# An fp32 attention block: the last product of each four-group stream moved one half block, and the last additions issued singly

## The chip, the cores and the metric

The kernel runs on one core of a Trainium2 chip. The metric is the device time of one execution in microseconds (us); before the change it is 3124.0 us, the median of three runs between 3122.99 and 3124.39.

## The reference, cut to what matters

The input is 16 images of 512 channels by 1024 positions, fp32. Each is normalised in 8 groups of channels, goes through one projection to q, k and v, attention with 4 heads of 128 channels, an output projection and the residual.

```python
xn  = groupnorm(x, 8) * gamma + beta              # x: (16, 512, 32, 32)
q, k, v = split(einsum('oc,bchw->bohw', qkv_w, xn) + qkv_b, 3)
attn = softmax(einsum('bhnd,bhmd->bhnm', q, k) * dh ** -0.5)
out  = einsum('bhnm,bhmd->bhnd', attn, v)          # 4 heads of dh = 128
return x + einsum('oc,bchw->bohw', proj_w, out) + proj_b
```

## The kernel before, in words

**Blocks and half blocks.** The spine of the program is a loop over 16 images x 4 heads x 8 key blocks. Each key block is done in two halves of 512 queries, called half blocks here. A half block issues one product of scores (tile `s`, line 1674, in `score`), its exponential on ScalarE (tile `p`, line 1680), and the weighted sum of the previous block (tile `po`, line 1771). VectorE adds up the exponentials once per block (tile `tot`, line 1695). A head has 16 half blocks, numbered 0 to 15.

**What runs between them.** All other products are put into these half blocks as units: one entry of the list `halfway` is run behind the `po` product of each half block. They are the q/k products of the next images, the v products, and the output projection of the image before (head 1, tiles `pp`). They use Strassen's scheme on two levels. Seven outer products are made in four groups (`OUTER = ((1, 5), (2, 6), (7, 4), (3,))`), and each group is a Strassen scheme of seven inner units in the order p1, p2, p6, p5, p7, p4, p3. From image 4 on, q, k and v come from another scheme instead (`thirds`, 16 groups, tiles `t_x`, `t_y`, `t_z`, line 1241), so four-group streams remain for the projection of every image but the last (15 of them), for v of images 1 to 3 (head 3 of the image before), and for the q/k products of images 1 to 3: the first pair in head 2 of the image before (stride 4), the second pair in head 0 (stride 3).

**The y bank.** Inside a group, p5 makes the bank y and p7 the bank x; VectorE adds both into the group's result (`out_`, line 817, here the first reading addition). Only then may p3 add its product onto y; VectorE reads y again behind it (the second reading addition, line 817). p3 of the last group is one instruction, `pp_y<-o` in the projection, 128 x 256.

**The order around the change.** `paced` puts the seven units of group g at the half blocks `stride * g + (0, 1, 1, 2, 2, 3, stride)`. With stride 3 and four groups the last entry is 12, and it holds both p4 and p3 of the last group:

```python
for k, i in enumerate((0, 1, 1, 2, 2, 3, stride)):
    at = halves_[stride * g + i]
    at.insert(1 if k == 0 and len(at) > 1 else len(at), us[k])
if stride == 4:
    carry.append(halves_.pop())
```

**Additions of whole blocks.** When a group is complete, `combine` queues additions of its results in the list `pending`. Each unit gives out one of them; in the last group of everything but v it gives out two; `end` gives out the rest. In the projection an output block (c11, c22, c21, c12) is finished by `finish`: the residual tile `y_c` plus one result (line 1648), plus the other (line 1649), then a DMA to the output on POOL's queue (line 1650). In v, `finish` is a VectorE scalar operation (line 1039), then `turn_v`: a transpose on VectorE (line 1046), a DMA to a scratch row, and four DMAs back. The tiles for these come from a pool of two.

**The next stream.** Head 2, behind the projection, starts `thirds` of the next image (from image 4 on). Its first group needs sums that VectorE makes in `home_A` (line 1159), its p3 is `t_y<-x`, and the second group's p2 is `t_z<-f`. ScalarE copies `t_x` into `t_z` (line 659) ahead of that p2. In the same stretch ScalarE issues the DMA of the softmax denominators (`row<-r`, line 1743), which waits for VectorE's reciprocal (line 1723).

Of the kernel before, what the change touches and what calls it, by code (L numbers as in the profile page):

```python
# [181 lines left out]
OUTER = ((1, 5), (2, 6), (7, 4), (3,))  # L182
# [49 lines left out]
def fast_path(ctx, tc, x, sources, out, consts, flag, dims):  # L232
# [6 lines left out]
    nc = tc.nc  # L239
# [150 lines left out]
    def own_t4(name="ot4"):  # L390
        t = tpool.tile([P, KC, HALF], F32, tag="ot4", name=name)
        return t
# [224 lines left out]
    ahead, inner_kept, late = {}, {}, {}  # L617

    def run(units):
        for u in units:  # L620
            u()
# [75 lines left out]
    def two_levels(name, site, b, blocks, finish, sums="make", homes="BBBB", prepare=None):  # L697
# [9 lines left out]
        opening = b == 0 and site == 0  # L707

        def placed():
            return tc.high_priority(URGENT) if opening else nullcontext()  # L710

        def part(g, i, row=None):
            t = R[g][:, i]
            return t if row is None else t[:, row, :]
# [42 lines left out]
        def group_units(g):  # L757
            group = OUTER[g]
            n = len(group)
# [82 lines left out]
            def unit(*steps):  # L842
                def one():
                    for f in steps:
                        f()
                    with placed():
                        for _ in range(min(len(pending), 2 if g == len(OUTER) - 1 and site != "v" else 1)):
                            pending.pop(0)()
                return one

            def end():
                combine(g)
                if g == len(OUTER) - 1:
                    with placed():
                        run(pending)
                    pending.clear()


# [9 lines left out]
                    first_keys if opening and g == len(OUTER) - 1 else lambda: None,  # L868
                ),
                unit(lambda: load("t3"), p4), unit(lambda: load("t4"), p3, end),  # L870
            ]

# [14 lines left out]
        pending = []  # L887
# [8 lines left out]

        def done(which, i, j):
            if prepare:
                pending.append(lambda: finish(which, part(*i), part(*j)))
                return  # L900
            pending.extend(
                lambda r=r: finish(which, r, part(*i, r), part(*j, r)) for r in range(2)
            )

        def combine(g):

            if g == 1 and opening:
                pending.append(lambda: result("c11", 0))
                add((1, 1), (0, 0), (1, 1), 0)
                add((1, 0), (1, 1), (0, 1), 0)  # L910


                def lower():
                    with tc.issue_after(latest["outer"].ins):
                        result("c11", 1)
                        nc.vector.tensor_add(part(1, 1, 1), part(0, 0, 1), part(1, 1, 1))

                pending.extend((lambda: None, lower))
            elif g == 1:
                done("c11", (0, 0), (1, 0))  # L920
                add((1, 1), (0, 0), (1, 1))
                add((1, 0), (1, 1), (0, 1))
            elif g == 2 and opening:
                add((2, 0), (1, 1), (2, 0), 0)
            elif g == 2:
                add((2, 0), (1, 1), (2, 0))
                done("c22", (2, 0), (0, 1))
                done("c21", (2, 0), (2, 1))
            elif g == 3 and opening:

                def rest():
                    result("c12", 0)
                    beside["scores"] = latest["result"]
                    with tc.issue_after(latest["result"].ins):
                        for o, i, j in (((1, 0), (1, 1), (0, 1)), ((2, 0), (1, 1), (2, 0))):
                            nc.vector.tensor_add(part(*o, 1), part(*i, 1), part(*j, 1))
                        for r in (1, 0):
                            result("c22", r)

                pending.append(rest)  # L940

                def second_head():
                    with tc.issue_after(latest["sum"].ins):
                        result("c21", 1)
                        result("c12", 1)

                beside["second head"] = second_head
            elif g == 3:
                done("c12", (1, 0), (3, 0))
# [28 lines left out]
    def qk_groups(b, pair):  # L978

        def finish(which, r, a, c):  # L980
            of, half = int(which[1]) - 1, int(which[2]) - 1
            st, h = (qs, ks)[of], 2 * pair + r
            head_tiles(b, pair)
            i = of * HEADS + h
            return nc.vector.scalar_tensor_tensor(
                st[b, h][:, ts(half, HALF)], a, qkb_sb[:, i : i + 1], c, ALU.add, ALU.add
            )

        return two_levels(
            f"qk_{b}_{pair}", pair, b, lambda: xb[b], finish,  # L990
            "make" if pair or b == 0 else "keep",
            "ABBB" if pair else "ABAB" if b > 0 else "BCBC",
        )
# [83 lines left out]
    def thirds(b):  # L1077
# [268 lines left out]
        def combine(G):  # L1346
# [88 lines left out]
            elif g == 7:  # L1435
                final(0, 0, True, 14, 13, (14, 13))
                op(True, 12, 12, 11, (11,))
                final(2, 1, False, 12, 9, (12, 9))

        return paced([group_units(G) for G in range(2 * count)], 3)  # L1440

    store3, builder = {}, {}
# [177 lines left out]
    def proj_groups(b):  # L1620

        ys = {}

        def place(which):
            row, half = int(which[1]) - 1, int(which[2]) - 1
            return lambda t: t[b, ts(row, KC * P), ts(half, HALF)].rearrange(
                "(r p) n -> p r n", p=P
            )

        def prepare(which):  # L1630
            own = which == "c12"
            t = ys[which] = own_t4(f"y_{b}_{which}") if own else ypool.tile(
                [P, KC, HALF], F32, tag="y", name=f"y_{b}_{which}"
            )
            eng = nc.sync if own else nc.gpsimd
            dma = eng.dma_start(t, place(which)(x))

            tc.add_manual_dep(
                dma.ins, last_eviction[b].ins.name,
                mybir.DependencyInfo(  # L1640
                    mybir.DependencyClass.Sync, mybir.DependencyReason.DATA
                ),
                reason="residual",
            )

        def finish(which, a, c):
            t = ys.pop(which)
            nc.vector.tensor_add(t, a, t)  # L1648
            nc.vector.tensor_add(t, t, c)  # L1649
            latest["sent"] = nc.gpsimd.dma_start(place(which)(out), t)  # L1650

        return two_levels(f"pp_{b}", "proj", b, lambda: ob[b], finish, prepare=prepare)


# [4 lines left out]
    def where(s):  # L1659
        bh, j = divmod(s, NB)  # L1660
        return (*divmod(bh, HEADS), j)
# [155 lines left out]
    def paced(groups, stride):  # L1817

        halves_ = [[] for _ in range(stride * len(groups) + 1)]
        for g, us in enumerate(groups):  # L1820
            for k, i in enumerate((0, 1, 1, 2, 2, 3, stride)):
                at = halves_[stride * g + i]
                at.insert(1 if k == 0 and len(at) > 1 else len(at), us[k])
        if stride == 4:
            carry.append(halves_.pop())
        return halves_

    def last_loads(what):
# [162 lines left out]
    def plan_head(b, h):  # L1991
# [9 lines left out]
        if h == 0:  # L2001
            if b > 0:
                if b < old:
                    spread(plan, [None] * 28, 0, NB)
                    halfway.extend(paced(next_qk.pop(), 3))
                plan[6].append(lambda: o_blocks(b - 1))
                plan[6].append(lambda: sums_of_b(ob[b - 1]))
                if old <= b < B - 1:
                    plan[5].append(lambda: load_x(b + 1, range(NCC)))
            else:  # L2010
                products(plan, staggered(next_qk.pop(), (0, 4, 8, 12)), 0)
                plan[1].append(beside["second head"])
                plan[3].append(lambda: load_x(1, range(KC)))
                for c in range(KC):
                    for half, step in enumerate(stats_steps(1, c)):
                        plan[4 + 2 * c].append(lambda step=step: behind_exp(step))
        elif h == 1:
            if b > 0:
                spread(plan, [None] * 28, 0, NB)
                halfway.extend(paced(proj_groups(b - 1), 3))  # L2020
                if flow:
                    halfway[0] = flow.pop() + halfway[0]
# [292 lines left out]
    with tc.issue_after(opened.ins):  # L2315
        run(units[3:-1])
        stage_sums(0)
        groups = [iter(units[-1:])] + [iter(us) for us in qk_groups(0, 0)]
# [13 lines left out]
    for s in range(steps + 1):  # L2332
        units = []
        if s < steps:
            b, h, j = where(s)
# [12 lines left out]
        for half in range(NH2):  # L2348
# [21 lines left out]
            n = (len(units) + 1) // 2  # L2370
# [158 lines left out]
```

## Time and profile before

| what | value |
|---|---|
| time, median of 3 runs | 3124.0 us |
| profiled execution, its own time | 3122.96 us |
| its span in the trace | 3121.4 us |
| TensorE (PE) matmul busy | 3106.9 us, 100% |
| PE weight loads busy | 2263.2 us, 73% |
| VectorE (DVE) busy | 2698.9 us, 86% |
| ScalarE (ACT) busy | 1722.7 us, 55% |
| GpSimd (POOL) busy | 469.7 us, 15% |
| one image from image 5 on | 192.75 us (the same row comes again at 1104.79 and 1297.54 us) |

The trace gives the start of each instruction, how long it was busy, and, in brackets, how long its engine had been idle before it and what ended that. One fp32 product shows as two matmul rows, so "x2" in a row of the timeline is one product. "PEld" is PE's weight load, "ACTq" ScalarE's queue, where it issues DMAs. 1.6 us of the execution lie around the span.

### The profile page before, as it was taken

What the parts mean: (1) busy time and instruction counts of PE and PEld (TensorE: products, weight loads), DVE (VectorE), ACT (ScalarE), POOL (GpSimd) and SP (SyncE); (2) the same over time, 40 slices, a digit from 0 to 9 for tenths busy, and PEclk for the clock granted to TensorE, in tenths of its full rate; (3) what the DMA queues carried; (4) which work ended last, traced back from release to release, by engine and by line L of the source; (5) the groups of instructions that cost most, each with busy time, mean ns of one, the idle gap of its engine ahead of it and who ended that gap; (6) DMA issues with size and microseconds to landing.
All of it is one profiled execution on the core that took longest, in us unless ns stands there. A gap on an engine that the chain in (4) does not pass through costs nothing.

```text
span 3121.4 us, 38228 instructions
## 1 busy us (share of the span) xinstructions
PE 3106.9 (100%) x11934; PEld 2263.2 (73%) x11934; DVE 2698.9 (86%) x4604; ACT 1722.7 (55%) x3744; POOL 469.7 (15%) x792
## 2 busy tenths in 40 slices
PE   9999999999999999999999999999999999999999
PEld 8567676677777777777777777777777777777775
DVE  9988988789898897988979889798898988989787
ACT  3545546455465655656556565565655656555543
POOL 0121121111111111211111111111111111111010
PEclk9999999999999999999999999999999999999999
DMA  5566765666767666666676666766667576675651
GB/s 177 174 227 194 249 206 192 210 196 213 235 212 221 193 209 222 205 212 198 202 221 209 212 202 204 224 202 211 200 202 230 196 219 200 210 223 191 222 194 42
DMA packets 244064, 636.80 MB, mean 204 GB/s; under 512 B 32656, under 2 KB 77840, under 8 KB 243856
## 3 DMA queue, kind: packets, MB, share of 16 engines
q1 hardware_dynamic: 164912, 363.58, 36.9%
q0 software_dynamic: 66272, 236.38, 22.3%
q10 hardware_dynamic: 12672, 34.35, 3.8%
q8 instruction: 96, 1.57, 0.2%
q14 instruction: 112, 0.92, 0.1%
HBM read 462.49 MB, written 171.69 MB: 203 GB/s over the span
## 4 chain that ended last, share of the span: by engine, by line
PE 67%; DVE 4%; issue 1%; ACT 0%; POOL 0%; ACTq 0%; DVEq 0%; POOLq 0%
PE po L1771 20%; PE s L1674 19%; PE t_x L1241 12%; PE t_y L1241 6%; PE pp_x L784 3%; PE t_z L1241 3%; PE pp_y L784 2%; PE pp_z L784 1%; DVE pp_r L817 1%; DVE pp_r L891 1%; DVE tot L1695 1%; DVE home_B L749 0%; DVE y_c L1649 0%; DVE y_c L1648 0%; DVE o L1784 0%
## 5 line engine op out<-in xcount | busy, mean ns | idle before, releaser
L1771 PE MATMUL po<-p,v 128*128 128x512 f32 x2048 | 1045.4, 592 | 0.0
L1674 PE MATMUL s<-qk,qk 128*128 128x512 f32 x2048 | 1045.2, 592 | 0.0
L1680 ACT ACTIVATE p<-s 128x512 f32<-128x512 f32 x1024 | 611.7, 597 | 509.2 <-PE s L1674 499.2
L1771 PEld LDWEIGHTS po<-p,v 128*128 128x128 f32 x2048 | 615.9, 301 | 374.9 <-issue 258.3
L1695 DVE TENSOR_TENSOR tot<-tot,p 128x1024 f32<-128x1024 f32 (+1 forms) x408 | 471.3, 1156 | 163.4 <-ACT p L1680 161.6
L1674 PEld LDWEIGHTS s<-qk,qk 128*128 128x128 f32 x2048 | 362.0, 189 | 58.9 <-issue 29.2
L1265 DVE TENSOR_TENSOR r<-t_y,t_u 128x342 f32<-128x342 f32 (+1 forms) x384 | 185.3, 482 | 138.7 <-PE t_y L1241 111.6
L1356 DVE TENSOR_TENSOR r<-r,r 128x684 f32<-128x684 f32 x264 | 225.8, 863 | 1.7
L1241 PE MATMUL t_x<-home_B,w 128*128 128x171 f32 x1008 | 187.7, 308 | 0.0
L1241 PE MATMUL t_x<-home_A,w 128*128 128x171 f32 x1008 | 187.6, 308 | 0.0
L1241 PEld LDWEIGHTS t_x<-home_B,w 128*128 128x128 f32 x1008 | 161.7, 189 | 30.2 <-issue 20.1
L1241 PEld LDWEIGHTS t_x<-home_A,w 128*128 128x128 f32 x1008 | 161.6, 189 | 30.2 <-issue 20.1
L784 PE MATMUL pp_x<-home_B,w_proj 128*128 128x256 f32 x630 | 166.0, 380 | 0.0
L1065 POOL DMA_DIRECT2D v<-vd x240 | 139.7, 589 | 148.8 <-DMA vd<-vu 55.7
L784 PEld LDWEIGHTS pp_x<-home_B,w_proj 128*128 128x128 f32 x630 | 119.2, 190 | 36.2 <-issue 12.6
L1128 DVE TENSOR_TENSOR f<-x 128x684 f32<-128x684 f32 x168 | 144.1, 858 | 0.8
L1201 ACT COPY t_u<-t_x 128x342 f32<-128x342 f32 x192 | 78.7, 410 | 119.0 <-PE t_x L1241 112.0
L293 POOL DMA_DIRECT2D x<-in_x x60 | 32.7, 548 | 640.2 <-PE t_x L1241 409.0
L1241 PEld LDWEIGHTS t_z<-f,w 128*128 128x128 f32 x528 | 89.5, 190 | 51.9 <-issue 34.3
L1326 DVE STREAM_TRANSPOSE vu<-vt 128x256 f32<-128x256 f32 x192 | 104.3, 643 | 0.0
L1207 ACT ACTIVATE t_u<-t_x,bias 128x171 f32<-128x171 f32 x192 | 72.2, 403 | 56.9 <-PE t_x L1241 56.9
L1166 POOL DMA_DIRECT2D kept_t<-home_A x96 | 52.4, 546 | 321.5 <-DVE home_A L1159 312.1
(383 smaller groups left out, 5153.7 us busy)
## 6 DMA issues: line engine op xcount, KB each, us to landing
w<-kept SPq DMA_DIRECT2D x182, 512.0 KB, 3.9
w<-kept SPq DMA_DIRECT2D x182, 384.0 KB, 4.1
kept_t<-home_A POOLq DMA_DIRECT2D x96, 342.0 KB, 3.8
home_B<-kept_t SPq DMA_DIRECT2D x96, 342.0 KB, 3.0
rinv<-row ACTq DMA_DIRECT2D x63, 512.0 KB, 4.8
x<-in_x POOLq DMA_DIRECT2D x60, 512.0 KB, 6.0
v<-vd POOLq DMA_DIRECT2D x240, 128.0 KB, 5.2
out_y<-y_c POOLq DMA_DIRECT2D x60, 512.0 KB, 3.9
```

Of the source, the lines that this page charges most:

```text
L784: latest["product"] = nc.tensor.matmul(acc[:, ts(i, Q)], have["w"][t][:, i, slot, :], inner(i, bn), start=(first and i == 0), stop=True, s ...
L1065: nc.gpsimd.dma_start(vs[b, pair][ts(q, BLK), half].rearrange("m h (k i) j -> m (h k) (i j)", k=n), rows.rearrange("(k m) (q e) -> q m k e ...
L1128: (eng.tensor_add if op == "+" else eng.tensor_sub)(made[f], of(a), of(c))
L1201: nc.scalar.copy(dst, src)
L1241: latest["product"] = nc.tensor.matmul(acc[:, ts(i, H3)], wts[G, t][:, i, slot, :], moving, start=(start and i == 0), stop=True, skip_grou ...
L1265: nc.vector.tensor_add(dst, view(a), view(c))
L1326: nc.vector.transpose(u[:, h].rearrange("p (q i j) -> p j q i", q=n, i=BLK)[:, ds(2 * q, 2)], made["vt"][:, h, ts(part, Q)].rearrange("p ( ...
L1356: (nc.vector.tensor_add if add else nc.vector.tensor_sub)(at(o), a, c)
L1674: latest["score"] = nc.tensor.matmul(sc, ks[b, h][:, ts(j, P)], qs[b, h][:, ts(half, HALF)], start=True, stop=True)
L1680: exps[s] = nc.scalar.activation(ps[s][:, ts(half, HALF)], sc, AF.Exp, scale=SCALE)
L1695: added[b, h, j] = nc.vector.tensor_add(tot[b, h][:, i], tot[b, h][:, i], ps[s][:, i])
L1771: summed = nc.tensor.matmul(po[half], v_block(b, h, j), ps[s][:, i], start=(j == 0), stop=(j == NB - 1),)
```

## The change

Four edits go together:

1. `paced`: for four groups with stride 3, p3 of the last group goes into an entry of its own, so that it runs in half block 13 instead of 12. This holds for the 15 projections, v of images 1 to 3 and the second q/k pair of images 1 to 3.
2. `done` and `finish`: in the projection the two additions of an output block are two entries of `pending` instead of one.
3. `unit`: in the last group one entry is given out per unit instead of two (the opening image keeps two).
4. `end`: what v still has pending at its end is appended to `late["tail"]`, which the main loop empties at the end of the half block, two entries each time.

```diff
-                        for _ in range(min(len(pending), 2 if g == len(OUTER) - 1 and site != "v" else 1)):
+                        n = 2 if opening and g == len(OUTER) - 1 else 1
+                        for _ in range(min(len(pending), n)):
                             pending.pop(0)()
...
                 if g == len(OUTER) - 1:
-                    with placed():
-                        run(pending)
+                    if site == "v":
+                        late["tail"] = late.get("tail", []) + pending
+                    else:
+                        with placed():
+                            run(pending)
                     pending.clear()
...
             if prepare:
-                pending.append(lambda: finish(which, part(*i), part(*j)))
+                pending.append(lambda: finish(which, part(*i), None))
+                pending.append(lambda: finish(which, None, part(*j)))
                 return
...
         def finish(which, a, c):
-            t = ys.pop(which)
-            nc.vector.tensor_add(t, a, t)
+            t = ys[which]
+            if c is None:
+                nc.vector.tensor_add(t, a, t)
+                return
             nc.vector.tensor_add(t, t, c)
             latest["sent"] = nc.gpsimd.dma_start(place(which)(out), t)
...
         if stride == 4:
             carry.append(halves_.pop())
+        elif len(groups) == len(OUTER):
+            halves_.append([halves_[-1].pop()])
         return halves_
```

Where the instructions stand is decided from these lists and from priorities, so three places show what moved. First PE in head 1 of image 5, at the end of the projection of image 4 (`pp_3_x` and `pp_3_y` are p4 and p3 of the last group; `s` and `po` belong to the half blocks). Before:

```order
L784 MATMUL pp_3_x<-home_B,w_proj_7644 128x256
L784 MATMUL pp_3_y<-o_3_7058,w_proj_7644 128x256
L1674 MATMUL s_1_7705<-qk_5_0_6547,qk_5_0_6548 128x512
L1771 MATMUL po_1_1_7479<-p_7660,v_0_6903 128x512
L1674 MATMUL s_0_7711<-qk_5_0_6547,qk_5_0_6548 128x512
```

After:

```order
L784 MATMUL pp_3_x<-home_B,w_proj_7644 128x256
L1681 MATMUL s_1_7700<-qk_5_0_6547,qk_5_0_6548 128x512
L1778 MATMUL po_1_1_7479<-p_7660,v_0_6903 128x512
L784 MATMUL pp_3_y<-o_3_7058,w_proj_7644 128x256
L1681 MATMUL s_0_7711<-qk_5_0_6547,qk_5_0_6548 128x512
```

The product onto y now stands behind the scores and the weighted sum of the next half block. In the projections of images 0 and 1 it stood between these two before, and stands behind both now.

Second, VectorE at the same place (`y_c` are the residual tiles, `pp_r_7420` with a `pp_3_y` are the two reading additions). Before:

```order
L1649 TENSOR_TENSOR y_c_7620<-y_c_7620,pp_r_7420 128x1024
L817 TENSOR_TENSOR pp_r_7420<-pp_3_y,pp_3_u_7687 128x256
L1649 TENSOR_TENSOR y_c_7622<-y_c_7622,pp_r_7586 128x1024
L1695 TENSOR_TENSOR tot_1_7475<-tot_1_7475,p_7660 128x1024
L817 TENSOR_TENSOR pp_r_7420<-pp_3_y,pp_3_u_7674 128x256
L1648 TENSOR_TENSOR y_c_7682<-pp_r_7514,y_c_7682 128x1024
L1695 TENSOR_TENSOR tot_1_7475<-tot_1_7475,p_7693 128x1024
L1649 TENSOR_TENSOR y_c_7682<-y_c_7682,pp_r_7420 128x1024
```

After:

```order
L1656 TENSOR_TENSOR y_c_7619<-y_c_7619,pp_r_7420 128x1024
L817 TENSOR_TENSOR pp_r_7420<-pp_3_y,pp_3_u_7685 128x256
L1702 TENSOR_TENSOR tot_1_7475<-tot_1_7475,p_7660 128x1024
L1656 TENSOR_TENSOR y_c_7621<-y_c_7621,pp_r_7584 128x1024
L1654 TENSOR_TENSOR y_c_7679<-pp_r_7514,y_c_7679 128x1024
L817 TENSOR_TENSOR pp_r_7420<-pp_3_y,pp_3_u_7669 128x256
L1702 TENSOR_TENSOR tot_1_7475<-tot_1_7475,p_7693 128x1024
L1656 TENSOR_TENSOR y_c_7679<-y_c_7679,pp_r_7420 128x1024
```

The first reading addition keeps its place; the second now has three long additions between it and the first instead of two. What stands ahead of these rows and behind them is unchanged.

Third, VectorE at the end of v for image 1, in head 3 of image 0 (`vt` are v's output tiles, `v_r_1508` with `v_3_y` the reading additions). Before:

```order
L817 TENSOR_TENSOR v_r_1508<-v_3_y,v_3_u_1758 128x256
L749 TENSOR_TENSOR home_A<-x,home_A 128x256 x2
L749 TENSOR_TENSOR home_B<-x 128x256
L1039 SCALAR_TENSOR_TENSOR vt_1_0_0_1752<-v_r_1668,vb_sb 128x512
L817 TENSOR_TENSOR v_r_1508<-v_3_y,v_3_u_1734 128x256
L1046 STREAM_TRANSPOSE vt_1_0_0_1752<-vt_1_0_0_1752 128x4x128
L1039 SCALAR_TENSOR_TENSOR vt_1_1_0_1761<-v_r_1668,vb_sb 128x512
L1695 TENSOR_TENSOR tot_3_1546<-tot_3_1546,p_1776 128x1024
L1046 STREAM_TRANSPOSE vt_1_1_0_1761<-vt_1_1_0_1761 128x4x128
```

After:

```order
L817 TENSOR_TENSOR v_r_1508<-v_3_y,v_3_u_1758 128x256
L749 TENSOR_TENSOR home_A<-x,home_A 128x256 x2
L749 TENSOR_TENSOR home_B<-x 128x256
L1044 SCALAR_TENSOR_TENSOR vt_1_0_0_1752<-v_r_1668,vb_sb 128x512
L1044 SCALAR_TENSOR_TENSOR vt_1_1_0_1761<-v_r_1668,vb_sb 128x512
L1051 STREAM_TRANSPOSE vt_1_0_0_1752<-vt_1_0_0_1752 128x4x128
L1051 STREAM_TRANSPOSE vt_1_1_0_1761<-vt_1_1_0_1761 128x4x128
L817 TENSOR_TENSOR v_r_1508<-v_3_y,v_3_u_1734 128x256
L1702 TENSOR_TENSOR tot_3_1546<-tot_3_1546,p_1776 128x1024
```

Here the second scalar operation and both transposes pass ahead of the second reading addition. On PE, `v_3_y` moves behind `s` and `po` as the projection's product does. On the queues of POOL and SP the DMAs stand in the same order as before, and on ScalarE one exponential of image 3 passes one normalisation.

## The prediction

> **What bounds the kernel.** I read the page's busy times first, then the list of who waited for whom on PE, and then the timeline at the waits it names.
>
> ```profile
> PE 3106.9 (100%) x11934; PEld 2263.2 (73%) x11934; DVE 2698.9 (86%) x4604; ACT 1722.7 (55%) x3744; POOL 469.7 (15%) x792
> ```
>
> ```profile
> PE pp_y L784 <- DVE pp_r L817: 4.4, 12, 0.4
> PE v_y L784 <- DVE v_r L817: 2.5, 3, 0.8
> ```
>
> PE is the bound: 3106.9 of 3121.4 us. No edit removes a product, so all that can be won is time in which PE stands still. Half of that is in these two rows, and both name the product that the change moves: `pp_y` of the projection stood 12 times for VectorE's first reading addition, `v_y` 3 times. This is one of the twelve, at the end of the projection of image 4:
>
> ```profile
> 1102.11 1.02 PE L1674 MATMUL s<-qk,qk 128*128 128x512 f32 x2
> 1102.97 1.02 PE L1771 MATMUL po<-p,v 128*128 128x512 f32 x2
> 1103.83 0.59 PE L784 MATMUL pp_x<-home_B,w_proj 128*128 128x256 f32 x2
> 1104.79 0.70 PE L784 MATMUL pp_y<-o,w_proj 128*128 128x256 f32 x2 [0.37 <-DVE pp_r L817]
> 1105.33 1.02 PE L1674 MATMUL s<-qk,qk 128*128 128x512 f32 x2
> ```
>
> A 512-wide product begins 0.86 us after the one before, so a 256-wide one takes its place for 0.43. From `pp_x` to the next `s` two of these should pass in 0.86; they took 1.50. The stop costs **0.64 us**, more than the 0.37 in brackets, since the product that waited also runs 0.11 longer (0.70 against 0.59). VectorE over the same time:
>
> ```profile
> 1103.18 1.22 DVE L1649 TENSOR_TENSOR y_c<-y_c,pp_r 128x1024 f32<-128x1024 f32 x1
> 1104.32 0.42 DVE L817 TENSOR_TENSOR pp_r<-pp_y,pp_u 128x256 f32<-128x256 f32 x1
> 1104.65 1.22 DVE L1649 TENSOR_TENSOR y_c<-y_c,pp_r 128x1024 f32<-128x1024 f32 x1
> 1105.79 1.22 DVE L1695 TENSOR_TENSOR tot<-tot,p 128x1024 f32<-128x1024 f32 x1
> 1106.92 0.42 DVE L817 TENSOR_TENSOR pp_r<-pp_y,pp_u 128x256 f32<-128x256 f32 x1
> 1107.26 1.22 DVE L1648 TENSOR_TENSOR y_c<-pp_r,y_c 128x1024 f32<-128x1024 f32 x1
> ```
>
> The addition that PE waited for began when a long one ended (1103.18, one every 1.14): VectorE was late, not its input. The busy times by stretch say for how long that holds:
>
> ```profile
> 1095.00:1130.00 35.00, 34.63 (x126) 24.25 (x125) 34.73 (x54) 21.34 (x42) 6.26 (x11) 1.00 0.63 203
> ```
>
> The columns behind 35.00 are PE, PEld, DVE, ACT and POOL. In these 35 us PE is busy for 34.63 and VectorE for 34.73: **two engines are full at once**, PE at full clock (1.00). That decides what the removed stop is worth.
>
> **The change, part by part.** *The projections of images 3 to 13 (eleven).* With `s` and `po` ahead, p3 begins at 1103.83 + 0.43 + 2 x 0.86 = 1105.98. The first reading addition ends at 1104.74 as before, so the stop is gone and PE is 0.64 ahead. VectorE is not: its list up to there is the same, and behind it stand the same operations in another order, so it does everything after 1110 at the same time as before. So I look at what PE next takes from VectorE's row. A wait costs nothing if it ends early enough: the addition ended at 1104.74, `pp_y` began 0.05 later and lost 0.11 more, so a release must come **0.16 ahead** of its product.
>
> ```profile
> 1113.78 0.51 DVE L1159 TENSOR_TENSOR home_A<-x,home_A 128x342 f32<-128x342 f32 x1
> ```
> ```profile
> 1115.07 0.31 PE L1241 MATMUL t_x<-home_A,w 128*128 128x171 f32 x1
> ```
>
> Ready at 1114.29, used at 1115.07: 0.78 ahead, so PE may come 0.62 earlier. This one takes almost nothing back.
>
> ```profile
> 1120.40 0.49 DVE L1265 TENSOR_TENSOR r<-t_y,t_u 128x342 f32<-128x342 f32 x1
> ```
> ```profile
> 1121.41 0.31 PE L1241 MATMUL t_y<-x,w 128*128 128x171 f32 x1
> ```
>
> Ready at 1120.89, used at 1121.41: 0.52 ahead, so 0.36 is kept. The last place goes through ScalarE:
>
> ```profile
> 1121.70 0.34 DVE L1723 RECIPROCAL r<-l 32x32 f32<-32x32 f32 x1
> ```
> ```profile
> 1122.07 0.36 ACTq L1743 DMA_DIRECT2D row<-r  x1
> 1122.47 0.45 ACT L1201 COPY r<-t_x 128x342 f32<-128x342 f32 x1 [2.29 <-PE t_y L1241]
> 1122.82 0.45 ACT L659 COPY t_z<-t_x 128x342 f32<-128x342 f32 x1
> ```
> ```profile
> 1123.71 0.31 PE L1241 MATMUL t_z<-f,w 128*128 128x171 f32 x1
> ```
>
> ScalarE issues the DMA of the denominators, which needs VectorE's reciprocal (ended 1122.04), and two copies stand behind it. `t_z` is ready at 1123.27 and used at 1123.71: 0.44 ahead, so **0.28 is kept**. VectorE first waits for PE again here:
>
> ```profile
> 1130.25 0.52 DVE L1159 TENSOR_TENSOR home_B<-f,home_B 128x342 f32<-128x342 f32 x1 [0.39 <-PE t_x L1241]
> ```
>
> With 0.39 of idle ended by PE, from here VectorE comes earlier by what PE has kept, and nothing more is lost. Eleven times 0.28 is **3.1 us** of the 7.0 removed. Bounds: 0.17 each if the late row costs a second start (2 us), 0.36 if ScalarE's copies come early (4 us).
>
> The Trainium skill, PSUM — Partial Sum Buffer, section Engine vs sequencer instructions, says that ScalarE's queue is strictly first in, first out. By that rule the copies cannot pass the waiting DMA issue; the rows at 1122.07 and 1122.47 agree, one following the other. Could they pass, this term would be 4.0 and the sum 0.9 more.
>
> *v of images 1 to 3.* The stop of the first one:
>
> ```profile
> 224.15 0.59 PE L784 MATMUL v_x<-home_B,w_v 128*128 128x256 f32 x2
> 225.59 0.70 PE L784 MATMUL v_y<-x,w_v 128*128 128x256 f32 x2 [0.84 <-DVE v_r L817]
> 226.13 1.02 PE L1674 MATMUL s<-qk,qk 128*128 128x512 f32 x2
> ```
>
> 1.98 instead of 0.86: 1.12 us, and the like for the others (the list above has 2.5 in three). VectorE is full again behind it, and in each of the three another row gives time back:
>
> ```profile
> 241.01 0.59 ACT L643 COPY qk_u<-qk_x 128x512 f32<-128x512 f32 x1
> ```
> ```profile
> 242.46 0.38 PE L784 MATMUL qk_x<-home_A,w 128*128 128x256 f32 x1
> ```
> ```profile
> 438.64 0.69 DVE L817 TENSOR_TENSOR qk_r<-qk_y,qk_u 128x512 f32<-128x512 f32 x1
> ```
> ```profile
> 440.31 0.38 PE L784 MATMUL qk_y<-x,w 128*128 128x256 f32 x1
> ```
> ```profile
> 637.06 1.13 PE L784 MATMUL qk_y<-x,w 128*128 128x256 f32 x4 [0.22 <-DVE qk_r L817]
> ```
>
> Image 1: ready 241.60, 0.86 ahead, 0.70 kept. Image 2: ready 439.33, 0.98 ahead, 0.82 kept at most. Image 3: PE waits for VectorE there already, so nothing is kept. The new order also brings v's second scalar operation forward to a wait on a DMA:
>
> ```profile
> 422.95 0.75 DVE L1039 SCALAR_TENSOR_TENSOR vt<-v_r,vb_sb 128x512 f32<-128x512 f32 x1 [0.31 <-DMA vd<-vt]
> ```
>
> The first of the pair waits 0.31 for its tile of the pool of two. The transfer for the second was issued one transpose later, so I take up to 0.3 more of VectorE's time; behind it are the reading addition, `tot` and the next q/k additions. Image 2 then keeps between 0.5 and 0.82. Together I take **1.4 us** (bounds 0.7 and 2.1).
>
> *The projections of images 0 to 2.*
>
> ```profile
> 323.19 1.02 PE L1674 MATMUL s<-qk,qk 128*128 128x512 f32 x2
> 324.21 0.70 PE L784 MATMUL pp_y<-o,w_proj 128*128 128x256 f32 x2
> 324.74 1.03 PE L1771 MATMUL po<-p,v 128*128 128x512 f32 x2
> ```
>
> Image 0 loses 0.26 here (1.55 instead of 1.29). The next stream takes its sums from VectorE soon after, so I take half for each of the first two and 0.1 for the third: **0.4 us** (bounds 0 and 1.2).
>
> *At nothing.* The halved additions are the same instructions, only given out singly; the q/k stream loses nothing to a stop now and keeps its products. The output DMAs keep their places on POOL's queue and leave at most about 2 us later; their tiles are next needed in the next projection, most of 192 us on. The second reading addition waits for the moved product: queued behind it are `tot` and the last residual addition. VectorE reaches it at 1104.65 + 3 x 1.14 = 1108.07; the product begins at 1105.98 and ends by 1106.57. That leaves 1.5 us, and if it were gone VectorE's row would be late one for one.
>
> The sum is 3.1 + 1.4 + 0.4 = 4.9. The profiled execution took 3122.96 (span 3121.4 and 1.6 around it), giving 3118.1; it lies 1.04 below the median of the runs, so on their scale the forecast is **3119.1 us**, 0.16% faster. About 0.2% (6.2 us) is what a measurement of this kernel can tell from no change.
>
> **The rivals.** *A, the forecast: removed, more than half given back.* Own range 3117.0 (4.0 + 2.1 + 0.9) to 3121.2 (2.0 + 0.7 + 0.1). 70%.
>
> *B, the whole stop is kept:* 11 x 0.64 + 3 x 1.12 + 1.2 = 11.6, 3112.4 us. It needs VectorE to get ahead too. Against it: 34.73 busy in 35.00. 12%.
>
> The Trainium skill, Perfetto Trace Analysis, section Tensor Engine Instruction (MATMUL, LD_WEIGHTS), says that the end of a matmul in the trace is computed from its size, only its start is observed. By idle times, which use these ends, B would be worth 4.4 + 2.5 = 6.9; by starts, 0.64 against 0.37 a piece, it is 11.6. The rows side with starts here (1.50 for 0.86).
>
> *C, all is given back:* VectorE's row, not PE's, sets the time through the whole stretch, and the stops turn up again at `t_y` and `t_z`: 3123 to 3124. For it: `t_y` has only 0.52. Against: that is more than 0.16. 13%.
>
> *D, slower:* VectorE stands at the second reading addition for the moved product. It decides from the point where the product ends after 1108.07; each us of standing is a us of VectorE's full row, of which PE is spared 0.28 an image. If nothing stood between the two additions, VectorE would arrive at 1104.74 and stand 1.83: 11 x 1.55 = 17 us, 3141. The order of the changed kernel has three long additions there. 5%.
>
> The range should reach over A and C: 3116.5 to 3124.0; B and D, 17%, stay out. Faster by over 0.2%: B and the fast end of A, 22%. Slower: most of D, 4%. The rest 74%.
>
> **What would show it.** The waits of PE for the reading additions of `pp_y` and `v_y` should be gone from PE's list. In their place `t_y` and `t_z` should show stops of 0.1 to 0.3 us eleven times, and an image should take 192.45 instead of 192.75 us. `qk_y` of image 3 should wait about 1.1 us longer. If the period falls by 0.6, VectorE was not full and B holds; if VectorE shows idle time ended by PE's `pp_y`, D holds; if the period stays, C.

## The result, and the profile after

The changed kernel takes **3119.17 us** (median of 20 runs, 3117.96 to 3120.96) against 3123.48 before (20 runs); the ratio is 0.9985, interval 0.9978 to 0.9992. The forecast was 3119.1. The traced execution took 3120.19 us, with a span of 3118.6; it lies 1.0 above its median, where that of before lay 0.5 below.

The page's busy times and PE's waits after the change (us in total, times, longest):

```profile
PE 3107.3 (100%) x11934; PEld 2263.5 (73%) x11934; DVE 2698.4 (87%) x4604; ACT 1718.8 (55%) x3744; POOL 469.6 (15%) x792
```
```profile
PE t_y L1246 <- DVE r L1270: 2.2, 2, 1.6
PE qk_x L784 <- ACT qk_u L643: 2.1, 2, 1.3
PE warm L2133 <- DVE avg L309: 1.6, 1, 1.6
PE qk_y L784 <- DVE qk_r L817: 1.2, 2, 1.0
```

The work is the same; both groups that the change aimed at, `pp_y` and `v_y`, are gone from the list. New are `qk_x` and a longer `qk_y`, behind v. The end of the projection of image 4, PE first and then VectorE:

```profile
1104.50 0.59 PE L784 MATMUL pp_x<-home_B,w_proj 128*128 128x256 f32 x2
1104.93 1.02 PE L1681 MATMUL s<-qk,qk 128*128 128x512 f32 x2
1105.79 1.02 PE L1778 MATMUL po<-p,v 128*128 128x512 f32 x2
1106.65 0.59 PE L784 MATMUL pp_y<-o,w_proj 128*128 128x256 f32 x2
```
```profile
1104.99 0.42 DVE L817 TENSOR_TENSOR pp_r<-pp_y,pp_u 128x256 f32<-128x256 f32 x1
...
1108.72 0.42 DVE L817 TENSOR_TENSOR pp_r<-pp_y,pp_u 128x256 f32<-128x256 f32 x1
```

From `pp_x` each product takes 0.43 or 0.86; nothing stands still. The moved product ends at 1107.24 and VectorE comes to it at 1108.72, 1.5 later, as forecast. Seventeen us on, VectorE, PE and ScalarE in the next stream:

```profile
1121.08 0.49 DVE L1270 TENSOR_TENSOR r<-t_y,t_u 128x342 f32<-128x342 f32 x1
```
```profile
1120.88 0.74 PE L1246 MATMUL t_x<-f,w 128*128 128x171 f32 x4
1121.63 0.85 PE L1246 MATMUL t_y<-x,w 128*128 128x171 f32 x4
1122.32 1.02 PE L1681 MATMUL s<-qk,qk 128*128 128x512 f32 x2
```
```profile
1122.74 0.32 ACTq L1750 DMA_DIRECT2D row<-r  x1
1123.10 0.45 ACT L1206 COPY r<-t_x 128x342 f32<-128x342 f32 x1 [2.86 <-DVE r L1730]
1123.44 0.45 ACT L659 COPY t_z<-t_x 128x342 f32<-128x342 f32 x1
```
```profile
1124.03 0.77 PE L1246 MATMUL t_z<-f,w 128*128 128x171 f32 x4
```

Four 171-wide products pass in 0.58 where nothing stops them (4 x 0.145). From `t_x` to `t_y` it is 0.75, and from `t_y` to `s` 0.69 (the product that waited ran 0.85, not 0.74): **0.28 us** given back, because the addition ends at 1121.57. PE's list of waits does not have this stop; it shows only from start to start. `t_z` is ready at 1123.89, 0.14 ahead, and begins on time, 0.86 behind the product before it; its four products then pass in 0.61 instead of 0.58, so 0.03 goes here. Of 0.64, 0.28 and 0.03 are given back and 0.33 is kept. In the next image the same row reads:

```profile
1314.05 0.85 PE L1246 MATMUL t_y<-x,w 128*128 128x171 f32 x4
```

1314.05 - 1121.63 = **192.42 us per image**, against 192.75 before and 192.45 forecast.

### The profile page after: what moved, and what is told of

Read it like the earlier page. It is cut to its first block, busy times and chain, and to the rows that moved or that the text cites. A ratio compares the mean times of both kernels' runs of the same rounds, so it can differ in the third digit from the quotient of the medians.

```text
span 3118.6 us, 38227 instructions
## 1 busy us (share of the span) xinstructions
PE 3107.3 (100%) x11934; PEld 2263.5 (73%) x11934; DVE 2698.4 (87%) x4604; ACT 1718.8 (55%) x3744; POOL 469.6 (15%) x792
## 3 DMA queue, kind: packets, MB, share of 16 engines
q8 instruction: 96, 1.57, 0.2%
## 4 chain that ended last, share of the span: by engine, by line
PE 72%; DVE 0%; issue 0%
PE po L1778 21%; PE s L1681 21%; PE t_x L1246 12%; PE t_y L1246 6%; PE pp_x L784 5%; PE t_z L1246 3%; PE pp_y L784 2%; PE pp_z L784 1%; PE lx L1898 0%; PE lv L1898 0%; PE last_x L784 0%; PE lz L1898 0%; PE lw L1898 0%; PE last_y L784 0%; PE last_z L784 0%; DVE r L1270 0%
```

## The experiments

Theory 1: what the change wins comes from the projections of images 3 to 13, and VectorE's full row behind them gives half of it back at `t_y`, with `t_z` next to it. Its rivals: v wins as forecast (theory 2); the stop at `t_y` has another cause (theory 3). Theories 4 and 5 on v's transfers came up on the way.

Beside the time, each trace gives PE's position: the start of a product of scores (`s`) less that of the same one before the change. The table shows by how much it moved over a stretch (plus is later): over v of images 1, 2 and 3; over the projections of images 0 to 2; over the start of `thirds` (column "image 4"), from head 3 of image 3 to the first half blocks of head 1 of image 4; and, as a mean per image, over the projections of images 3 to 13. Times are medians; the first row has 20 runs, the others 8 to 11.

| run | v 1 | v 2 | v 3 | proj. 0-2 | image 4 | each of 3-13 | us | ratio to before |
|---|---|---|---|---|---|---|---|---|
| the change | +0.44 | +0.66 | -0.12 | -0.59 | +0.51 | -0.33 | 3119.17 | 0.9985 |
| after_again | -1.11 | +0.62 | -0.08 | -0.58 | +2.89 | -0.33 | 3119.64 | 0.9985 |
| move_only | +0.33 | +0.25 | -0.08 | -0.53 | +1.28 | -0.30 | 3119.93 | 0.9987 |
| proj_only | -0.04 | 0.00 | +0.04 | -0.56 | +1.71 | -0.33 | 3120.23 | 0.9989 |
| v_only | +0.35 | +0.53 | -0.12 | -0.23 | +1.24 | 0.00 | 3124.36 | 1.0001 |
| dose_034 | -0.30 | +0.63 | -0.14 | +1.30 | +0.12 | -0.03 | 3124.95 | 1.0005 |
| v_behind | -0.81 | +0.11 | -0.02 | -0.57 | +1.65 | -0.32 | 3119.85 | 0.9986 |
| forms_late | -0.83 | +0.29 | -0.11 | -0.56 | +0.47 | -0.60 | 3116.62 | 0.9978 |
| best1 | 0.00 | +0.01 | +0.05 | -0.29 | +0.35 | -0.62 | 3116.57 | 0.9978 |
| best2 | -0.48 | +0.43 | -0.02 | -0.55 | +0.81 | -0.61 | 3117.14 | 0.9979 |
| fetch_after | -0.38 | -0.85 | -0.12 | -0.75 | +2.77 | -0.33 | 3119.84 | 0.9985 |
| fetch_forms | -0.01 | -0.82 | -0.11 | -0.31 | -0.27 | -0.58 | 3116.65 | 0.9978 |
| fetch_best | -0.61 | -0.85 | -0.03 | -0.59 | +0.54 | -0.59 | 3115.23 | 0.9974 |

Each ratio's interval reaches 0.0007 to 0.0011 to either side, some 2 to 3.4 us, so the traces carry the terms below that.

**proj_only: the projections alone.**

```diff
-        elif len(groups) == len(OUTER):
+        elif split:
...
-                halfway.extend(paced(proj_groups(b - 1), 3))
+                halfway.extend(paced(proj_groups(b - 1), 3, True))
...
-                        n = 2 if opening and g == len(OUTER) - 1 else 1
+                        n = 2 if g == len(OUTER) - 1 and (opening or not prepare and site != "v") else 1
```

> The move and the single additions in the projections alone; v and the q/k products as before the change. Theory 1 (what is won is won in the projections of images 3 to 13, 0.33 us each, and the move in v loses: in the trace of the change PE is 0.44 us later over v of image 1, 0.66 later over image 2, 0.13 earlier over image 3): v's net loss of 1.0 goes, so 1.0 us under the change, about 3118.2, and PE's waits at qk_x and qk_y of images 1 to 3 are those of before. Theory 2 (v's loss was the luck of one execution and v wins 1.4 as forecast): 1.4 us above the change, 3120.6.

A row of PE's waits in its trace:

```profile
PE v_y L784 <- DVE v_r L817: 2.5, 3, 0.9
```

PE's three stops at `v_y` are back, and each image from 5 on wins the same 0.33. But the time is 3120.2, not 3118.2, and so next to theory 2's 3120.6: v's stretches are at zero, and the start of `thirds` took 1.7 us. The "net loss of 1.0" in v that I read from one trace is no property of the change: after_again has -0.57 in all for v where the change's trace had +0.98.

**v_only: v alone.** The projections' additions are whole again and two of them given out per unit, as in move_only below.

```diff
-        elif len(groups) == len(OUTER):
+        elif split:
...
-            halfway.extend(paced(next_v.pop(), 3))
+            halfway.extend(paced(next_v.pop(), 3, True))
```

> The move in v of images 1 to 3 alone; the projections and the q/k products as before the change. Theory 1 (VectorE's second scalar operation now waits for the DMA of the one but last tile of v, and all of it reaches PE): PE's three waits at v_y (2.5 us) are gone, but about 1.0 us is lost net behind them, so 1 us above before, 3124.5. Theory 2 (the forecast's term): 1.4 us under before, 3122.1.

VectorE at the end of v for image 2:

```profile
424.61 1.42 DVE L1046 SCALAR_TENSOR_TENSOR vt<-v_r,vb_sb 128x512 f32<-128x512 f32 x2 [1.68 <-DMA vd<-vt]
```

3124.36, ratio 1.0001 with an interval from 0.9992 to 1.0010: v alone wins nothing that can be measured, as theory 1 had it (3124.5). The two times point to different theories, since the stretch at image 4 is in both (+1.71 and +1.24). What decides is the column of images 3 to 13: 0.33 a piece with the projections moved, 0.00 without. VectorE stands 1.68 us at image 2 for the DMA of a tile of v; before it stood 0.31 (the row at 422.95 in the prediction).

**dose_034: 0.335 us more on VectorE.**

```diff
             nc.vector.tensor_add(t, t, c)
+            if which == "c12":
+                q = t[:, 0, :Q]
+                nc.vector.tensor_max(q, q, q)
```

> The change with one operation more on VectorE behind the last residual addition of each projection: the maximum of 128x256 elements with themselves (0.335 us from start to start), so the result is the same. Theory 1 (VectorE's row is full there, and sets PE's stop at t_y): each image takes 192.43 + 0.33 = 192.76 us, the stop at t_y grows by 0.33, and eleven images add 3.7 us to the change, about 3122.9. Theory 3 (the stop at t_y is PE's or ScalarE's own and VectorE has room): no difference, 3119.2.

PE in the stretch of `t_x` and `t_y` behind the projection of image 4:

```profile
1116.34 0.85 PE L1246 MATMUL t_x<-home_A,w 128*128 128x171 f32 x4
...
1122.95 0.85 PE L1246 MATMUL t_y<-x,w 128*128 128x171 f32 x4
```

An image takes 192.72 us, 0.30 more than the change, for 0.335 more on VectorE. The stop at `t_y` keeps its length and a second one appears ahead of it, at the `t_x` that reads `home_A`; a product that waited shows by its 0.85. The early projections pay as well (+1.30 for -0.59). In the trace this is 3.9 us; the median came out 5 to 6 above the change. VectorE's row sets what is given back, nearly one for one; theory 3 is out.

**forms_late: the same work, VectorE's row reordered.** `invert` holds the transpose and the reciprocal of the denominators; it now runs after the reading addition, and the two sums `f` behind it.

```diff
-            nc.vector.transpose(l[:, 3, :], l[:, 2, :])
-            nc.vector.reciprocal(r, l[:, at, :])
+                with tc.issue_after(latest["read"].ins) if behind_read else nullcontext():
+                    nc.vector.transpose(l[:, 3, :], l[:, 2, :])
+                latest["turned"] = nc.vector.reciprocal(r, l[:, at, :])
...
+                late_ = G == 2 and b > old
+                with tc.issue_after(latest["turned"].ins) if late_ else nullcontext():
                     (eng.tensor_add if op == "+" else eng.tensor_sub)(made[f], of(a), of(c))
```

> The change with VectorE's row in another order and with no less work: behind each projection from image 4 on, the first reading addition of t_y comes ahead of two sums f, and the reciprocal of the denominators ahead of them too. By durations of the trace t_y is then released 0.8 us earlier and t_z 1.2 us. Theory 1 (those two places hold back what the projection wins): the stops at t_y are gone, an image takes 192.12 to 192.16 us instead of 192.43, and the time is 3 to 3.4 us under the change, about 3116. Theory 3 (something else that cannot come earlier stands right behind, such as a load of weights or ScalarE's copies): the stop only moves on, 192.43 and 3119.2.

VectorE, then PE, at the same place:

```profile
1118.14 0.49 DVE L1272 TENSOR_TENSOR r<-t_y,t_u 128x342 f32<-128x342 f32 x1
1118.57 0.19 DVE L1737 STREAM_TRANSPOSE l<-l 32x32 f32<-32x32 f32 x1
1118.79 0.34 DVE L1738 RECIPROCAL r<-l 32x32 f32<-32x32 f32 x1
```
```profile
1119.32 0.74 PE L1248 MATMUL t_y<-x,w 128*128 128x171 f32 x4
1119.89 1.02 PE L1685 MATMUL s<-qk,qk 128*128 128x512 f32 x2
1120.75 1.02 PE L1791 MATMUL po<-p,v 128*128 128x512 f32 x2
1121.61 0.74 PE L1248 MATMUL t_z<-f,w 128*128 128x171 f32 x4
```

The addition ends 0.69 ahead of `t_y`, and both products run 0.74: no stop. An image takes 192.12 us, 0.63 under before (one of the eleven, image 8, only 0.28), so the whole stop is kept, and the time is 3116.62. What held back half the gain in these images was VectorE's row at these two places. The run clears both at once; the 0.28 and 0.03 of the change's trace tell them apart.

**move_only: the first edit alone.** `both` runs the two calls of `finish` one behind the other.

```diff
-                pending.append(lambda: finish(which, part(*i), None))
-                pending.append(lambda: finish(which, None, part(*j)))
+                pending.append(both)
...
-                        n = 2 if opening and g == len(OUTER) - 1 else 1
+                        n = 2 if g == len(OUTER) - 1 and site != "v" else 1
...
-                    if site == "v":
-                        late["tail"] = late.get("tail", []) + pending
-                    else:
-                        with placed():
-                            run(pending)
+                    with placed():
+                        run(pending)
```

> The first edit alone: the product moved; whole additions, two of them given out per unit in the last group, and v's rest issued where it was before. On VectorE three long additions stand between the two reading additions as in the change, only in another order. Theory 1: the other three edits are worth nothing, the time is that of the change, 3119.2, an image takes 192.43 us and the stops at t_y are 0.27 long. Rival: the single additions carry part of it; then the time lies between the change and before, 3120 to 3123.

3119.93 (ratio 0.9987) beside 3119.17 and 3119.64 for the change (0.9985 both), and in ten of the eleven images the same 0.33. The other three edits are worth nothing that shows here.

**v_behind: v's second scalar operation behind the second reading addition.** In v's last group p7 and p4 give out no entry, so that it stands behind p3 in the program.

```diff
+            second = (pair, h, half) == (1, 1, 0)
+            with tc.issue_after(latest["outer"].ins) if second else nullcontext():
                 nc.vector.scalar_tensor_tensor(t, a, vb_sb[:, i : i + 1], c, ALU.add, ALU.add)
```

> The change, but in v of images 1 to 3 the second scalar operation is put behind the second reading addition, so that VectorE meets the wait for the second tile of the pool 2.5 to 3 us later. Theory 4 (v loses at image 2 because VectorE stands 1.4 to 1.8 us for the transfer of the second tile, where it stood 0.31 before): the wait shrinks to about 0.3, PE's step over the start of image 2's next head falls from +1.7 to about +0.4, and the time is about 1.3 us under the change, 3117.9. Rival (PE's step there comes from ScalarE's copy or the order of the q/k stream): the step stays at 1.4 to 1.7, 3119.2.

VectorE at the end of v for image 2:

```profile
423.16 0.75 DVE L1048 SCALAR_TENSOR_TENSOR vt<-v_r,vb_sb 128x512 f32<-128x512 f32 x1 [1.32 <-DMA vd<-vt]
```

Theory 4 falls: the first of the two operations stands 1.32 us, alone, so the order of the pair is not what makes VectorE stand. PE's step over the start of the next head, 1.8 in the change's trace, is 1.2, between the two forecasts (0.4, and 1.4 to 1.7). The transfer itself lands late. Here are the DMAs over the 3.6 us behind the issue of the first transfer, before and after the change (queue: packets, MB, share of 16 engines; then the median us from issue to landing):

```profile
q0 software_dynamic: 159, 0.52, 38.5%
q1 hardware_dynamic: 129, 0.46, 31.7%
...
vd<-vt POOLq DMA_DIRECT2D x2, 256.0 KB, 3.3
```
```profile
q0 software_dynamic: 151, 0.50, 36.3%
q1 hardware_dynamic: 126, 0.45, 35.1%
q8 instruction: 1, 0.02, 1.7%
...
vd<-vt POOLq DMA_DIRECT2D x2, 256.0 KB, 4.5
```

One packet is new, of the queue "instruction", and it takes 1.7% of 16 x 3.6 us = 1.0 us of one DMA engine, in the middle of the transfer; the two transfers land 1.2 us later. The page has 96 such packets, 1.57 MB, so 16 KB each, and PE has 2 x 11934 rows: one packet for some 250 of PE's instructions. It hangs on PE's place in its program. With the stop at `v_y` gone PE is over 1 us further when VectorE sends v's tiles, and the packet falls 2.3 us behind the issue; before, it came at 3.8, when the first of the two, which VectorE waits for, had landed (3.2). The ten traces up to here agree: in the seven with v moved the transfers take 4.1 to 4.5 us and VectorE stands 1.3 to 1.8; in the three with v as before (before, proj_only, best1) 3.1 to 3.3 and 0.3.

**after_again, fetch_after: the packet moved.** The first is the change once more; the second leaves out six warm-up products at the very start, which nothing reads, to shorten PE's program by 24 instructions.

```diff
-        warm(9, "warm_0")
+        warm(3, "warm_0")
```

> The change once more, beside the next two on the same chip, for a second trace. Theory 5 (the queue q8 brings PE's instructions 16 KB at a time, one packet in about 250 instructions; with the move in v, PE is so far ahead of VectorE at image 2 that a packet falls into the transfers of v's tiles and holds one of the 16 DMA engines for 0.95 us): the packet again begins 1.8 to 2.3 us behind the issue of the transfer at about 420, the transfers land 4.1 to 4.5 us after their issue, VectorE stands 1.3 to 1.8 us, and PE's step is +1.4 to +1.8. Time 3119.2 to 3120.

> The change with six of the nine products of the opening's first warm-up left out, whose result nothing reads: PE's program is 24 instructions shorter there, and no other engine's order changes. Each later packet of instructions is then asked for 24 instructions, about 3 us, later in the work. Theory 5: at image 2 it falls behind the transfers of v's tiles (4.8 us or more behind the issue, where they are over at 3.6); they land in 3.1 to 3.4 us, VectorE stands 0.3 to 0.6 and not 1.3 to 1.8, PE's step at the start of image 2 falls to about +0.4, and the time is 1.0 to 1.3 us under the change. Rival (the transfers are slow for another reason, such as the loads of weights beside them): 4.1 us or more to landing, and no difference in time.

VectorE at image 2 in the two, and the transfers of fetch_after over the same 3.6 us:

```profile
423.04 1.42 DVE L1044 SCALAR_TENSOR_TENSOR vt<-v_r,vb_sb 128x512 f32<-128x512 f32 x2 [1.75 <-DMA vd<-vt]
```
```profile
423.48 1.42 DVE L1044 SCALAR_TENSOR_TENSOR vt<-v_r,vb_sb 128x512 f32<-128x512 f32 x2 [0.29 <-DMA vd<-vt]
```
```profile
q0 software_dynamic: 160, 0.52, 37.9%
q1 hardware_dynamic: 137, 0.50, 36.9%
...
vd<-vt POOLq DMA_DIRECT2D x2, 256.0 KB, 3.1
```

Theory 5 holds at this place: the packet is out of the stretch (3.9 us behind the issue, for 2.25 in after_again), the transfers land in 3.1, VectorE stands 0.29, PE's step is +0.27 (after_again +1.74), and v of image 2 wins 0.85 instead of losing 0.62. The packet moved by 1.7 us and not the 3 expected, which was just enough. The time did not follow, since the opening pays. PE stands idle where the warm-up was:

```profile
PE pm L2163 <- DVE st L2223: 2.4, 1, 2.4
```

Its first scores begin 1.06 us later than before (in fetch_forms 1.67; by which step was not followed), and at image 4 this execution lost 2.8 in waits at `t_y`.

Elsewhere the packet weighs less. In the fourteen traces, 144 transfers have such a packet under way 1 to 3 us behind their issue in at least three traces, and none in at least three others. With it 106 of the 144 land later; the median over all is 0.33 us. And a transfer can be slow without it: v's next two, at 427, land at 5.1 in fetch_after for 3.2 to 4.1 before, with no such packet beside them.

**best1, best2, fetch_forms: combinations.** best1 is forms_late with v as before, best2 forms_late with v_behind, fetch_forms forms_late with the shorter warm-up; their edits are those above.

> The new order of VectorE's row of the run forms_late, with the move in the projections alone; v and the q/k products as before the change. The stops at t_y and t_z stay away, an image takes 192.12 us. Against forms_late (3116.6) it lacks what v's move is worth: 0.3 us lower or higher by the four traces so far (they show v at +0.27, -0.70 and the like), so 3116.3 to 3117; if v is worth the forecast 1.4, 3118.

> The new order of VectorE's row of the run forms_late, with v's second scalar operation behind the second reading addition as in v_behind. Theory 1 and theory 4 together: 3.2 us for the first and 1.3 for the second under the change, 3114.7; if theory 4 is wrong, 3116.6 as in forms_late.

> The run forms_late (VectorE's row in the new order) with the same six warm-up products left out. Theory 1 with theory 5: 1.0 to 1.3 us under forms_late (3116.6), about 3115.5, and the best of all; if theory 5 is wrong, 3116.6. If the first warm-up was needed for the clock, the opening takes longer and both runs with it left out lie above.

All three keep the 0.6 per image and stand at 3116.6 to 3117.1, like forms_late. best2 missed its 3114.7: with theory 4 wrong there was nothing to add. fetch_forms won 0.82 at image 2 and paid 1.7 at the opening.

**fetch_best: the packet moved at no cost.** On forms_late, the warm-up's nine products of 128 columns are written as three of 384.

```diff
-        warm(9, "warm_0")
+        warm(3, "warm_0", 3)
```

> The run forms_late with the nine products of the opening's first warm-up, 128 columns wide, written as three of 384 columns: the same work for PE, in 24 instructions less. Theory 5: the packet of instructions falls behind the transfers at image 2 as in fetch_after (VectorE stands 0.3 us, PE's step about +0.3), and the opening takes no longer than before (PE's wait at pm stays away, the first scores begin at 58.2 to 58.4 us and not at 59.3 to 60.0). The time is 1.1 us under forms_late, 3115.5, and the lowest of all. If the opening still takes 1.1 to 1.6 us longer, it was not the warm-up's length that mattered, and the time is 3116.6.

PE's first rows, and VectorE at image 2:

```profile
1.64 3.96 PE L2146 MATMUL warm<-avg 128*128 128x384 f32 x6 [1.64 <-DVE avg L309]
```
```profile
422.30 1.41 DVE L1044 SCALAR_TENSOR_TENSOR vt<-v_r,vb_sb 128x512 f32<-128x512 f32 x2 [0.27 <-DMA vd<-vt]
```

The warm-up takes as long as before, the opening is unchanged (-0.03), VectorE stands 0.27, and v wins 0.61 + 0.85 + 0.03. **3115.23 us**, ratio 0.9974 (0.9963 to 0.9984): the lowest median, 4 us under the change. Its interval overlaps that of forms_late; the 1.4 us between the two rest on the traces, where v of image 2 is at -0.85 and not +0.29.

## Why the prediction was right, point by point

*The stop and its price.* Forecast 0.64 by starts, 0.37 by idle times. `pp_x` begins 0.67 later than before (1104.50 for 1103.83), the next scores 0.40 earlier (1104.93 for 1105.33); of these 1.07, 0.43 is the product that moved, and 0.64 the stop. forms_late kept 0.63 an image. The reading by starts was the right one, in line with what is said in the Trainium skill, Perfetto Trace Analysis, section Tensor Engine Instruction (MATMUL, LD_WEIGHTS), that ends are computed.

*The give-back.* Right in its mechanism: VectorE's times did not move (the addition that releases `t_y` begins at 1120.40 before and 1121.08 after, 0.68 later, as the first reading addition does ahead of the place: 1104.32 and 1104.99). dose_034 and forms_late show that this row decides. The size was a little off: `t_y` took the 0.28 that its margin of 0.36 implies, and `t_z`, expected to leave only 0.28, took 0.03 more: 0.33 was kept, 11 x 0.33 = 3.6 for 3.1. (With 0.28 kept an image takes 192.47 us; the 192.45 of the forecast is a slip.) A release 0.14 ahead cost 0.03 at `t_z`, where I asked for 0.16. ScalarE's copies followed its DMA issue one for one, as assumed.

*v of images 1 to 3.* Here it was wrong in size. Forecast 1.4 won; the two traces of the change have 1.0 lost and 0.6 won. The stop at `v_y` did go: over the head that makes v PE gains 1.1 for each of the three images. The step that failed is what VectorE's waits for DMAs take back. At image 2, "I take up to 0.3 more of VectorE's time" became 1.4 to 1.5, through PE's packet of instructions. With the packet out of the way, in three runs, image 2 wins 0.82 to 0.85 (forecast 0.5 to 0.82) and image 3 0.03 to 0.12 (forecast 0). Image 1 wins 0.01, 0.38 and 0.61 in them, for 0.70, and went from -1.11 to +0.44 between the two traces of the change. There the forecast had no term for another wait of VectorE for a DMA, in head 0: 0 in the three traces with v as before, 0.9 to 2.2 with v moved. The longer it is, the less PE keeps, roughly; v_only alone is far off (+0.35 at 1.32). The two traces of the change:

```profile
262.35 0.43 DVE L1514 TENSOR_TENSOR a_o<-a_v 128x256 f32<-128x256 f32 x1 [2.21 <-DMA kepta<-a_o]
```
```profile
260.52 0.42 DVE L1514 TENSOR_TENSOR a_o<-a_v 128x256 f32<-128x256 f32 x1 [0.86 <-DMA kepta<-a_o]
```

*The projections of images 0 to 2.* 0.6 for 0.4. The traces do not fix it closer: v_only, which moves nothing there, has 0.23. (The forecast's own range takes 0.1 and 0.9 for this term, where its bounds were 0 and 1.2; with these it is 3116.7 to 3121.3.)

*The sum.* Forecast 3.1 + 1.4 + 0.4 = 4.9. The measured terms are 3.6 + 0.6, v between -1.0 and +0.6, and a term that I did not have: at image 4 PE stood 0.5 and 2.9 us longer in the two traces. So the sums of the traces are 2.7 and 2.0, and the medians moved by 4.3. That the time agrees to 0.1 us is luck in part: errors cancel, and the 0.6 by which the gain fell short of 4.9 is nearly the 0.5 by which the median of before fell from three runs (3124.0) to twenty (3123.48).

Two things make up the stretch at image 4. PE waits there at `t_y` for VectorE, which stands 1.8 to 3.5 us for a load of weights (2.3 before), and in all fourteen traces PE waits 1.0 to 1.1 less than VectorE stood. Why the load lands so differently is not settled. The second is PE's clock. In three traces (after_again, proj_only, v_behind) the granted clock fell to 0.50 for 3.41 us, from 0.4 to 1.4 us behind the end of this wait on. This is after_again:

```profile
853.25 1.15 PE L1246 MATMUL t_y<-x,w 128*128 128x171 f32 x4 [2.51 <-DVE r L1270]
854.19 1.92 PE L1681 MATMUL s<-qk,qk 128*128 128x512 f32 x2
855.90 1.61 PE L1778 MATMUL po<-p,v 128*128 128x512 f32 x2
```

A 512-wide product takes 1.71 us from start to start instead of 0.86. In each of the three traces the fall lies 846.5 us behind the clock's rise at the start, 248 times 3.4133. Cut from that rise into stretches of this length, PE stands 1.88 to 2.51 us of one stretch in these three, and up to 1.76 in ten others; only move_only, with 1.90 and no fall, does not fit neatly. The 2.38 us of v_only fall on two stretches (0.66 and 1.72) and leave the clock at 1.00. So what seems to count is how long PE stands within one stretch. This is read from the traces; no run was made on it. 3.41 us at half clock cost PE 1.7 us, of which 0.8 comes back at the next wait of `t_y`: 0.9 in each of the three. It weighs on the medians too: in every kernel that has executions with a mean granted clock of 0.999 (one to five), their median lies 0.3 to 3.5 us above that of the others; fetch_best has none.

*At nothing.* Right, as far as move_only tells, for the halved additions and v's tail, and for the second reading addition (1.5 us of cover, as forecast). The slower rival never came near its point. The stop of 1.1 us expected at `qk_y` of image 3 appeared earlier, at `qk_x` (0.79, and 0.16 at `qk_y`).

## What to carry to other kernels

When a stop is removed beside a second engine that is full, look up what the first engine next takes from the second one's row: the margins there bound what will be kept (0.36 and 0.28 here, and 0.33 was kept), and putting those operations ahead of work that nobody waits for can return the rest. A term of one us read from one trace is not yet a property of the kernel: a second trace of the same program moved it by more than its size, and one look at the granted clock around the stretch tells whether the products themselves ran slower. And an engine that comes earlier also brings its own fetches earlier, to where they may meet another engine's transfers.

## What was not expected of the hardware

PE's instructions come as DMA packets of 16 KB, which the page counts on the same 16 DMA engines as the data. The Trainium skill, Runtime: NRT & Kernel Launch, section Instruction fetch mechanics, says that the instruction memory is refilled in 16 KiB blocks of 256 instructions and that crossing a block is mostly hidden. The block agrees with the trace (96 packets, 1.57 MB). PE's lists show no wait for it, but its neighbours paid: one packet took 1.0 us of a DMA engine, the two 256 KB transfers at image 2 that it fell into landed at 4.1 to 4.5 us instead of 3.0 to 3.3, and 1.1 to 1.5 us of PE's time there hung on 24 instructions at the start of the program.
